# Softmax-window sums laid out as the image is, and the padding zeros of all images written early from another queue

## The chip, the cores and the metric

The kernel runs on one core of a Trainium2 chip. The metric is the device time of one execution in microseconds. The engines are called PE (matmul), DVE (vector), ACT (activations), POOL (GpSimd) and SP (which only issues DMAs here). Names such as L691 are lines of the kernel before.

## The reference

Two layers on x of shape (4, 16, 256, 256), each with a residual and a group norm in front of it (8 groups of two channels).

```python
# layer 0: x = x + L0(gn(x)); K = 5
out = conv3x3(h, conv_w) + conv_b                     # 16 -> 16*25 channels
weights = softmax(out.reshape(N, C, 25, H, W), axis=2)
y = einsum('ncuij,ncuij->ncij', unfold5x5(h), weights)
# layer 1: x = x + L1(gn(x)); a 3x3 KAN convolution
y = conv3x3(silu(h), base_weight.sum) + conv3x3(b_splines(h), (spline_weight * spline_scaler).sum) + bias_weight
```

In layer 0 each pixel and channel so needs a numerator (the sum over 25 taps of exp(logit) times the shifted h) and a denominator (the sum of the 25 exponentials). Both convolutions pad h with zeros.

## The kernel before

**Prologue.** The four images of x are read once for the group statistics (`bn_stats`, `group_stats`, whose L155 on POOL makes the reciprocal deviation), and bounds on the logits are taken. The weights are put in place by `prepare0` and `prepare1` (POOL: L471 and L472 copy the convolution's weights, L494 multiplies the spline's; ACT's `whi`, L474, and DVE's `wn`, L475, split one part in two). Image 0 is normalized here by the generator `normalize`, a step at a time between the statistics of the other images.

**What `normalize` writes.** It stores h three times into DRAM: `hs`, by strips with two rows and columns of padding, from which the shifted h is read; and `hst` and `hsl`, transposed by columns, from which the matmuls' operands are read. Its rows of zeros around h are DMAs of their own at the head of the generator: four into `hs` (L256), four into `hst` (L262) and four into `hsl` (L263), twelve for an image. Image 0's are issued from POOL's queue, in the prologue. Those of images 1, 2 and 3 are issued from SP's queue when layer 0 begins the image before, just ahead of the load of the first rows of x for the next image (`xp`, L276).

**Layer 0.** There are 64 strips: image, half of the rows (128 partitions), 32 columns. A strip has eight steps of four columns. In a step PE makes the logits of four columns (L791 with fp32 weights, L795 with the rest), ACT the exponentials into `e[:, 0]` (L814), POOL the products with h in `e[:, 1]` (L819), and DVE sums the 25 taps of both halves into `nd` (L691):

```python
nd = ndp.tile([P, 2, SW, C], F32, name=f"nd_{n}{arm}", tag="nd")
```

`nd` has three buffers and `e` four. After the last step of a strip, some steps later each, ACT computes a reciprocal of the denominators through Ln and Exp into the PSUM tile `r` (L704, L705), DVE corrects it by one Newton step (L709, L710) and multiplies the numerators by it (L713). This last multiply reads `nd` in its order, columns outside and channels inside, and writes the tile `o` in the order of x, channels outside:

```python
o = ndp.tile([P, C, SW], F32, name=f"o_{n}{arm}", tag="o", bufs=2)
nc.vector.tensor_mul(o.rearrange("p c j -> p j c"), nd[:, 1], r)
after(LAG + 3, apply, n, o, xc)
```

POOL subtracts `o` from x in `apply` (L719; the correction has the opposite sign), ACT takes statistics for layer 1 (L731), and every four strips ACT's queue stores the result (`x1s`). Between the steps of a strip run the steps of `normalize` for the next image: ACT normalizes, PE transposes, ACT copies, DVE subtracts (L366). Image 3 has no next image.

**Layer 1** follows; it computes splines on DVE and ACT and convolves on PE.

**What sets the order.** Within a layer the instructions of each engine are kept in the order of the program (`in_order`); in the prologue a scheduler orders them. SP's queue takes its DMAs in order, and so does POOL's, among POOL's arithmetic. A DMA waits for the one eight before it on the same kind of queue to land, as the two share a semaphore.

Of the kernel before, what the change touches and what calls it, by code (L numbers as in the profile page):

```python
# [11 lines left out]
F32 = mybir.dt.float32  # L12
# [21 lines left out]
def conv_preact_kernel(  # L34
# [12 lines left out]
    nc = tc.nc  # L47
    B, C, H, W = x.shape
    G = 8
    GC = C // G  # L50
    P = 128
    NH = H // P
# [3 lines left out]
    PAD = K // 2  # L56
    HP = H + 2 * PAD
    NS = 8
    EPS = 1e-5
    SW = 32  # L60
    NST = W // SW
    SP = SW + 2 * PAD
    CI = 8
    CX = 128
    JG = 4
    LAG = 1
    RP = P + 2
# [15 lines left out]
    hs = [dram.tile([NST, HP, C, SP], F32, name=f"hs{b}") for b in range(B)]  # L83
    hst = [[dram.tile([C, CT], F32, name=f"hst{b}_{h}") for h in range(NH)] for b in range(B)]

    hsl = [[dram.tile([C, 2, CT], F32, name=f"hsl{b}_{h}") for h in range(NH)] for b in range(B)]
# [38 lines left out]
    for r in range(RT):  # L125
        p = SROWS.index(r + 1) * C
# [115 lines left out]
    zero = const.tile([PAD * C, max(RP, NST * SP)], F32, name="zero")  # L242
# [2 lines left out]
    zpad = const.tile([P, QC, PAD], F32, name="zpad")  # L245
    nc.vector.memset(zpad, 0.0)

    def normalize(b, ptr, tiles, held=None, copier=None, queue=nc.sync):

        prep, xps, tts, his, los = tiles
        copier = copier or nc.scalar.copy
        for e in (0, HP - PAD):
            for r in range(PAD):
                queue.dma_start(  # L256
                    hs[b][:, e + r].rearrange("s c w -> c s w"),
                    zero[0:C, 0 : NST * SP].rearrange("c (s w) -> c s w", s=NST),
                )
        for h in range(NH):  # L260
            for w in (0, (W + 1) * RP):
                queue.dma_start(hst[b][h][:, w : w + RP], zero[0:C, 0:RP])  # L262
                queue.dma_start(  # L263
                    hsl[b][h][:, :, w : w + RP].rearrange("c t r -> (c t) r"), zero[:, 0:RP]
                )

        moves = []

        def move():
# [113 lines left out]
        for q in range(C // QC):  # L383
            ahead = rows(q + 1) if q + 1 < C // QC else iter(())
# [15 lines left out]
    with tc.tile_pool(name="prep0", bufs=2) as prep, tc.tile_pool(  # L400
        name="pre", bufs=1
    ) as pre, tc.tile_pool(
        name="xin", bufs=3
    ) as xin, tc.tile_pool(name="stat", bufs=2) as stat, tc.tile_pool(
        name="pstat", bufs=1, space=PSUM
    ) as pstat, tc.tile_pool(name="ptr0", bufs=3, space=PSUM) as ptr0:

        tiles = norm_tiles(prep)
        held = [pre.tile([P, C, W + 2 * PAD], F32, name=f"held{h}") for h in range(NH)]
# [15 lines left out]
        for dj in range(3):  # L425
            v = conv_wt[dj].rearrange("(d c) n -> c d n", d=3)
# [5 lines left out]
        v = conv_wt[2, 2 * C : 3 * C]  # L432
# [10 lines left out]
        for d in range(3):  # L443
# [3 lines left out]
            v = spl_s[dc]  # L447
# [73 lines left out]
        ahead = iter(())  # L521
        for b in range(B):
            st = stat.tile([P, G, NH * (GC if b == 0 else 1), 6], F32, name=f"st0_{b}", tag=f"st0{min(b, 1)}")
            for hf in range(NH):
                n = b * NH + hf
                t = loaded.pop(0)
                for g in range(G):
                    if b == 0:
                        for k in range(GC):
                            nc.vector.bn_stats(st[:, g, hf * GC + k, :], t[:, g * GC + k, :])  # L530
                    else:
                        nc.vector.bn_stats(
                            st[:, g, hf, :],
                            t[:, g * GC : (g + 1) * GC, :].rearrange("p c w -> p (c w)"),
                        )
                    next(ahead, None)
                    next(ahead, None)

                nc.scalar.activation(xq, t, AF.Square)
                sq = pstat.tile([P, W], F32, name=f"sq_{n}", tag="sq")  # L540
                for c in range(C):
                    nc.tensor.matmul(
                        sq, lhsT=idr, rhs=xq[:, c], start=c == 0, stop=c == C - 1
                    )
                nc.vector.tensor_reduce(hm[:, n : n + 1], sq, AX.X, ALU.max)
                next(ahead, None)
                if n >= NH and n + 3 < B * NH:
                    loaded.append(load_x(n + 3))
            mean, rstd = group_stats(stat, pstat, st, f"x{b}")
            nc.vector.tensor_copy(nrm[b][:, 0], rstd)  # L550
            nc.vector.scalar_tensor_tensor(nrm[b][:, 1], mean, -1.0, rstd, ALU.mult, ALU.mult)
            nc.gpsimd.tensor_mul(nrz[b][:, 0], rstd, gsel_sb)
            nc.vector.scalar_tensor_tensor(nrz[b][:, 1], rstd, EPS, rstd, ALU.mult, ALU.mult)
            ms = stat.tile([P, 2], F32, name=f"ms_{b}", tag="ms")
            nc.vector.tensor_mul(mean, mean, mean)
            nc.vector.tensor_reduce(ms[:, 0:1], mean, AX.X, ALU.add)
            nc.vector.tensor_scalar(ms[:, 0:1], ms[:, 0:1], 9.0 * GC, None, ALU.mult)
            nc.vector.tensor_reduce(ms[:, 1:2], rstd, AX.X, ALU.max)
            nc.vector.tensor_mul(ms[:, 1:2], ms[:, 1:2], ms[:, 1:2])
            v = hm[:, b * NH : (b + 1) * NH]  # L560
            nc.vector.tensor_scalar(v, v, 9.0 / 8.0, ms[:, 0:1], ALU.mult, ALU.add)
            nc.vector.tensor_scalar(v, v, ms[:, 1:2], None, ALU.mult)
            if b == 0:
                prepare0()
            if b == 1:
                prepare1()
            if b == 0:
                ahead = normalize(0, ptr0, tiles, held, nc.vector.tensor_copy, nc.gpsimd)
                next(ahead)
        for _ in ahead:  # L570
            pass
# [39 lines left out]
    def layer0(shift):  # L611

        arm = "g" if shift else ""
        marks = {}
        first = len(nc.cur_bb.bb.instructions)
        with tc.tile_pool(name=f"prep{arm}", bufs=2) as prep, tc.tile_pool(
            name=f"im{arm}", bufs=NIM
        ) as imp, tc.tile_pool(name=f"l0{arm}", bufs=2) as l0, tc.tile_pool(
            name=f"nd{arm}", bufs=3
        ) as ndp, tc.tile_pool(name=f"x1{arm}", bufs=3) as x1p, tc.tile_pool(name=f"ptr{arm}", bufs=1, space=PSUM) as ptr, tc.tile_pool(  # L620
            name=f"plog{arm}", bufs=3, space=PSUM
# [5 lines left out]
            tiles = norm_tiles(prep)  # L627
# [51 lines left out]
            def after(k, f, *args):  # L679

                later.append([k, partial(f, *args)])
# [7 lines left out]
            def sums():  # L689
                nd, j, e, done = waiting.pop(0)  # L690
                nc.vector.tensor_reduce(  # L691
                    nd[:, :, j : j + JG, :], e.rearrange("p t j m c d -> p t j c m d"),
                    AX.XY, ALU.add,
                )
                if done is not None:
                    done()

            def finish(n, nd, xc):
                after(LAG + 2, seed, n, nd, xc)


            def seed(n, nd, xc):
                r = prc.tile([P, SW, C], F32, name=f"r_{n}{arm}", tag="r")
                nc.scalar.activation(r, nd[:, 0], AF.Ln)  # L704
                nc.scalar.activation(r, r, AF.Exp, scale=-1.0)  # L705
                after(1, divide, n, nd, xc, r)

            def divide(n, nd, xc, r):
                nc.vector.tensor_mul(nd[:, 0], nd[:, 0], r)  # L709
                nc.vector.scalar_tensor_tensor(r, nd[:, 0], 2.0, r, ALU.subtract, ALU.mult)  # L710

                o = ndp.tile([P, C, SW], F32, name=f"o_{n}{arm}", tag="o", bufs=2)
                nc.vector.tensor_mul(o.rearrange("p c j -> p j c"), nd[:, 1], r)  # L713
                after(LAG + 3, apply, n, o, xc)

            def apply(n, o, xc):
                w0 = strips[n][2] * SW % CX
                v = xc[:, :, w0 : w0 + SW]
                nc.gpsimd.tensor_sub(v, v, o)  # L719
                if w0 + SW == CX:  # L720
                    for g in range(G):
                        after(1 + g, statistics, n, xc, g)
                    after(2, store, n, xc)
# [12 lines left out]
            def store(n, xc):  # L736
# [8 lines left out]
                    name=nc.get_next_instruction_name(), engine=mybir.EngineType.Activation,  # L745
# [8 lines left out]
            nxc, xc = load_xc(0), None  # L754
            ahead = iter(())
            for n, (b, hf, s) in enumerate(strips):
                if (hf, s) == (0, 0):
                    for _ in ahead:
                        pass
                    ahead = normalize(b + 1, ptr, tiles) if b + 1 < B else iter(())  # L760
# [8 lines left out]
                if s * SW % CX == 0:  # L769
                    xc = nxc  # L770

                nd = ndp.tile([P, 2, SW, C], F32, name=f"nd_{n}{arm}", tag="nd")
                for j in range(0, SW, JG):
                    if j % CI == 0:
                        k = n * nci + j // CI
# [10 lines left out]
                    e = l0.tile([P, 2, JG, K, C, K], F32, name=f"e_{n}_{j}{arm}", tag="e", bufs=LAG + 3)  # L786
                    for j1 in range(0, JG, 2):
                        lg = plog.tile([P, 2, 512], F32, name=f"lg_{n}_{j}_{j1}{arm}", tag="lg")
                        for i in range(2):
                            o = (j + j1 + i) % CI * RP  # L790
# [9 lines left out]
                        if shift:  # L800
                            mx = l0.tile([P, 2, C], F32, name=f"mx_{n}_{j}_{j1}{arm}", tag="mx")
                            for i in range(2):
                                v = lg[:, i, :NL].rearrange("p (m c d) -> p m c d", m=K, c=C)
# [3 lines left out]
                                w = bass.AP(  # L807
                                    tensor=mx.tensor, offset=mx.offset + i * C,
                                    ap=[mx.ap[0], [0, K], [1, C], [0, K]],
                                )  # L810
# [24 lines left out]
            while waiting:  # L835
                sums()
# [224 lines left out]
    with tc.If(fast > 0) as small_logits:  # L1061
        layer1("", *layer0(False))
    with small_logits.Else():
        layer1("g", *layer0(True))
# [42 lines left out]
```

## Time and profile before

| | us |
|---|---|
| median of 3 runs (lowest to highest) | 3093.68 (3092.81 to 3095.0) |
| the profiled execution | 3092.67 |
| its span | 3090.9 |
| of it: prologue, to the first reduce L691 | 135.8 |
| layer 0, first L691 to the last L713 | 135.8 to 2073 |
| layer 1 and the end | 2073 to 3091 |

The span is the time from the first to the last instruction of the profile. A group's row in the profile reads: line, engine, operation, tiles written and read, shapes and count; then busy time in us and mean ns of one; then the engine's idle time just before such instructions and what ended it. A timeline's row has start and duration in us, and in brackets the engine's idle time before it. SPq is SP issuing DMAs.

### The profile page before, as it was taken

How to read it: one execution, taken by the hardware profiler on the slowest of the kernel's cores; microseconds unless marked ns; L12 is line 12 of the kernel's file. 1: busy time of each engine (PE TensorE's matmuls, PEld its weight loads, DVE VectorE, ACT ScalarE, POOL GpSimd, SP SyncE). 2: the span in 40 equal slices, each digit the busy share in tenths (PEclk: the TensorE clock that was granted, in tenths of full speed). 3: DMA queues.
4: the chain of work that ended last, by engine and by line, in shares of the span. 5: the costliest groups of instructions: out<-in, count | busy, mean ns of one | idle time of the engine just before them, and what ended most of it. 6: DMA issues, size and time to landing. Idle time of an engine off the chain costs nothing.

```text
span 3090.9 us, 40797 instructions
## 1 busy us (share of the span) xinstructions
PE 2840.5 (92%) x14760; PEld 1484.6 (48%) x14760; DVE 2976.4 (96%) x1571; ACT 2240.5 (72%) x2619; POOL 1951.1 (63%) x734
## 2 busy tenths in 40 slices
PE   4499999989999999999999999957999999999998
PEld 3366656656556666666666566632222222222222
DVE  7499999999999999999999999988999999999997
ACT  6466665676766566756646546559999999999995
POOL 4199999999999999999999999970100100000000
PEclk7699999999999999999999999988999999999999
DMA  9988977879878778878867667649999988999994
GB/s 275 284 222 224 249 203 206 219 189 255 230 206 240 191 202 224 242 214 218 221 161 199 164 171 193 156 110 201 194 193 197 197 194 191 197 196 198 193 198 89
DMA packets 352725, 626.36 MB, mean 203 GB/s; under 512 B 41330, under 2 KB 218724, under 8 KB 336644
## 3 DMA queue, kind: packets, MB, share of 16 engines
q1 hardware_dynamic: 318020, 605.29, 79.0%
q10 hardware_dynamic: 33024, 16.78, 1.9%
q8 instruction: 121, 1.98, 0.3%
q0 software_dynamic: 1472, 1.59, 0.2%
q14 instruction: 88, 0.72, 0.1%
HBM read 513.95 MB, written 104.24 MB: 200 GB/s over the span
## 4 chain that ended last, share of the span: by engine, by line
DVE 65%; PE 9%; ACT 9%; issue 8%; DMA 6%; SPq 2%; POOL 1%; DVEq 0%; ACTq 0%; POOLq 0%
DVE nd L691 45%; PE yp L988 3%; PE lg L791 3%; DVE ta L169 3%; DVE ta L168 3%; DVE tb L169 3%; DVE tb L168 3%; DMA sx<-x1s 2%; DVE ring L170 2%; DVE o L713 1%; DVE tb L159 1%; DVE r L710 1%; DMA an<-hsl 1%; ACT sl L924 1%; ACT ta L167 1%
## 5 line engine op out<-in xcount | busy, mean ns | idle before, releaser
L791 PE MATMUL lg<-wm,am 128*128 128x400 f32 x4096 | 1741.2, 506 | 102.9 <-ACT e L814 64.2
L819 POOL TENSOR_TENSOR e<-e,u 128x1600 f32<-128x1600 f32 x512 | 1789.9, 3547 | 67.7 <-ACT e L814 48.6
L691 DVE TENSOR_REDUCE nd<-e 128x128 f32<-128x3200 f32 x512 | 1746.9, 3476 | 31.6 <-POOL e L819 31.5
L795 PE MATMUL lg<-wn,an 97*128 97x400 f32 x2048 | 1349.7, 659 | 12.1 <-DMA an<-hsl 11.9
L814 ACT ACTIVATE e<-lg 128x800 f32<-128x800 f32 x1024 | 817.8, 837 | 726.4 <-DVE nd L691 522.3
L791 PEld LDWEIGHTS lg<-wm,am 128*128 128x128 f32 x4096 | 764.3, 193 | 424.1 <-ACT e L814 113.3
L988 PE MATMUL yp<-ring,wt 128*32 128x512 f32 x6144 | 739.7, 595 | 66.8 <-POOL ring L959 46.5
L795 PEld LDWEIGHTS lg<-wn,an 97*128 97x128 f32 x2048 | 389.3, 190 | 330.3 <-issue 21.1
L988 PEld LDWEIGHTS yp<-ring,wt 128*32 128x32 f32 x6144 | 206.9, 109 | 591.5 <-issue 470.0
L905 POOL MEMSET sx<- 16x256 f32 x8 | 2.4, 302 | 667.2 <-PE yp L996 232.5
L1004 PE MATMUL yp<-sl,ws 64*32 64x512 f32 x1536 | 176.5, 588 | 0.0
L731 ACT ACTIVATE z<-xc,nrm 128x256 f32<-128x256 f32 x256 | 153.6, 600 | 10.5 <-POOL xc L719 6.2
L170 DVE SCALAR_TENSOR_TENSOR ring<-ta,ta 128x2048 f32<-128x2048 f32 (+1 forms) x64 | 147.8, 2309 | 10.8 <-ACT z L731 8.3
L169 DVE TENSOR_TENSOR ta<-ta,ta 128x2048 f32<-128x2048 f32 (+1 forms) x64 | 148.4, 2318 | 2.9 <-ACT ta L167 2.9
L170 DVE SCALAR_TENSOR_TENSOR ring<-tb,tb 128x2048 f32<-128x2048 f32 x64 | 145.6, 2276 | 2.6
L169 DVE TENSOR_TENSOR tb<-tb,tb 128x2048 f32<-128x2048 f32 x64 | 145.2, 2268 | 0.7 <-ACT tb L167 0.7
L924 ACT ACTIVATE sl<-sx,q 64x2048 f32<-64x2048 f32 x64 | 133.4, 2085 | 1.5 <-DMA sx<-x1s 1.4
L194 POOL TENSOR_TENSOR d<-d,nrz 128x8 f32<-128x8 f32 x4 | 2.7, 663 | 200.1 <-DVE d L192 200.1
L167 ACT ACTIVATE ta<-ta 128x2048 f32<-128x2048 f32 (+1 forms) x64 | 123.2, 1925 | 2.0
L167 ACT ACTIVATE tb<-tb 128x2048 f32<-128x2048 f32 x64 | 120.5, 1883 | 0.0
L1004 PEld LDWEIGHTS yp<-sl,ws 64*32 64x32 f32 x1536 | 48.8, 106 | 116.2 <-issue 115.9
L719 POOL TENSOR_TENSOR xc<-xc,o 128x512 f32<-128x512 f32 x64 | 85.0, 1328 | 13.4 <-DVE o L713 13.4
(181 smaller groups left out, 2054.3 us busy)
## 6 DMA issues: line engine op xcount, KB each, us to landing
am<-hst SPq DMA_DIRECT2D x512, 194.6 KB
u<-hs SPq DMA_DIRECT2D x320, 288.0 KB
an<-hsl SPq DMA_DIRECT2D x512, 129.8 KB
xta<-x1s SPq DMA_DIRECT2D x40, 1024.0 KB
xtb<-x1s SPq DMA_DIRECT2D x40, 1024.0 KB
xtc<-x1s SPq DMA_DIRECT2D x40, 1024.0 KB
am<-hst SPq DMA_DIRECT2D x256, 129.8 KB
sx<-x1s SPq DMA_DIRECT2D x248, 128.0 KB
```

The source lines that it names most:

```text
L167: nc.scalar.activation(s1, r1, AF.Square, scale=2.0)
L168: nc.vector.scalar_tensor_tensor(s2, t, 2.0, s2, ALU.subtract, ALU.mult)
L169: nc.vector.tensor_mul(s1, s1, r1)
L170: nc.vector.scalar_tensor_tensor(f, s2, 0.0, s1, ALU.min, ALU.subtract if given else ALU.add)
L691: nc.vector.tensor_reduce(nd[:, :, j : j + JG, :], e.rearrange("p t j m c d -> p t j c m d"), AX.XY, ALU.add,)
L791: nc.tensor.matmul(lg[:, i, :NL], lhsT=am[:, o : o + P], rhs=wm.rearrange("p m c d -> p (m c d)"), start=True, stop=False,)
L795: nc.tensor.matmul(lg[:, i, :NL], lhsT=an[:, o : o + P], rhs=wn.rearrange("p m c d -> p (m c d)"), start=False, stop=True,)
L814: nc.scalar.activation(ev, lg[:, :, :NL], AF.Exp)
L819: nc.gpsimd.tensor_tensor(e[:, 1].rearrange("p j m c d -> p j (m c) d"), e[:, 0].rearrange("p j m c d -> p j (m c) d"), uv, ALU.mult,)
L924: nc.scalar.activation(sl[n % 2][:, :, 1 : W + 1], t, AF.Silu, scale=sc[b][0][0 : RD * C], bias=sc[b][1][0 : RD * C],)
L988: nc.tensor.matmul(yp[t * M : (t + 1) * M], lhsT=wt[:, d, e].rearrange("p r o -> p (r o)"), rhs=ring[:, r0 + t * RT + d : r0 + t * RT + d ...
L1004: nc.tensor.matmul(yp[t * M : (t + 1) * M], lhsT=ws[:, e].rearrange("p r o -> p (r o)"), rhs=sl[n % 2][:, t : t + NT + 1 : NT, e : e + W], ...
```

## The change

`nd` is laid out as channels by columns, as x is, and so is `r`. L691 then writes its sums, which it still makes column by column, 32 elements apart. The last multiply runs in place in `nd`, `o` is gone, and `apply` reads `nd[:, 1]`. Apart from this, the zeros become a function of their own, `zeros(b)`, called in the prologue for each of the four images after its statistics and ahead of `prepare0` and `prepare1`, and all issued from POOL's queue.

```diff
+    def zeros(b):
+
         for e in (0, HP - PAD):
             for r in range(PAD):
-                queue.dma_start(
+                nc.gpsimd.dma_start(
                     hs[b][:, e + r].rearrange("s c w -> c s w"),
                     zero[0:C, 0 : NST * SP].rearrange("c (s w) -> c s w", s=NST),
                 )
         for h in range(NH):
             for w in (0, (W + 1) * RP):
-                queue.dma_start(hst[b][h][:, w : w + RP], zero[0:C, 0:RP])
-                queue.dma_start(
+                nc.gpsimd.dma_start(hst[b][h][:, w : w + RP], zero[0:C, 0:RP])
+                nc.gpsimd.dma_start(
                     hsl[b][h][:, :, w : w + RP].rearrange("c t r -> (c t) r"), zero[:, 0:RP]
                 )
 
+    def normalize(b, ptr, tiles, held=None, copier=None):
...
+            zeros(b)
             if b == 0:
                 prepare0()
             if b == 1:
                 prepare1()
             if b == 0:
-                ahead = normalize(0, ptr0, tiles, held, nc.vector.tensor_copy, nc.gpsimd)
+                ahead = normalize(0, ptr0, tiles, held, nc.vector.tensor_copy)
...
                 nc.vector.tensor_reduce(
-                    nd[:, :, j : j + JG, :], e.rearrange("p t j m c d -> p t j c m d"),
+                    nd[:, :, :, j : j + JG].rearrange("p t c j -> p t j c"),
+                    e.rearrange("p t j m c d -> p t j c m d"),
                     AX.XY, ALU.add,
                 )
...
-                r = prc.tile([P, SW, C], F32, name=f"r_{n}{arm}", tag="r")
+                r = prc.tile([P, C, SW], F32, name=f"r_{n}{arm}", tag="r")
...
-                o = ndp.tile([P, C, SW], F32, name=f"o_{n}{arm}", tag="o", bufs=2)
-                nc.vector.tensor_mul(o.rearrange("p c j -> p j c"), nd[:, 1], r)
-                after(LAG + 3, apply, n, o, xc)
-
-            def apply(n, o, xc):
+                nc.vector.tensor_mul(nd[:, 1], nd[:, 1], r)
+                after(LAG + 3, apply, n, nd, xc)
+
+            def apply(n, nd, xc):
                 w0 = strips[n][2] * SW % CX
                 v = xc[:, :, w0 : w0 + SW]
-                nc.gpsimd.tensor_sub(v, v, o)
+                nc.gpsimd.tensor_sub(v, v, nd[:, 1])
...
-                nd = ndp.tile([P, 2, SW, C], F32, name=f"nd_{n}{arm}", tag="nd")
+                nd = ndp.tile([P, 2, C, SW], F32, name=f"nd_{n}{arm}", tag="nd")
```

More of the change, by code (lines that the diff above doesn't have):

```diff
@@ L246, in conv_preact_kernel @@
     nc.vector.memset(zpad, 0.0)
-    def normalize(b, ptr, tiles, held=None, copier=None, queue=nc.sync):
-        prep, xps, tts, his, los = tiles
-        copier = copier or nc.scalar.copy
+    def zeros(b):
         for e in (0, HP - PAD):
             for r in range(PAD):
-                queue.dma_start(
+                nc.gpsimd.dma_start(
                     hs[b][:, e + r].rearrange("s c w -> c s w"),
@@ L261, in normalize @@
             for w in (0, (W + 1) * RP):
-                queue.dma_start(hst[b][h][:, w : w + RP], zero[0:C, 0:RP])
-                queue.dma_start(
+                nc.gpsimd.dma_start(hst[b][h][:, w : w + RP], zero[0:C, 0:RP])
+                nc.gpsimd.dma_start(
                     hsl[b][h][:, :, w : w + RP].rearrange("c t r -> (c t) r"), zero[:, 0:RP]
                 )
+    def normalize(b, ptr, tiles, held=None, copier=None):
+        prep, xps, tts, his, los = tiles
+        copier = copier or nc.scalar.copy
         moves = []
```

## The prediction

> **What bounds the kernel now.** I read the page first (busy times, then the slices), then the windows view by stage, then the groups with their shapes apart, and last the timelines of single engines where a stage begins.
>
> ```profile
> PE 2840.5 (92%) x14760; PEld 1484.6 (48%) x14760; DVE 2976.4 (96%) x1571; ACT 2240.5 (72%) x2619; POOL 1951.1 (63%) x734
> DVE  7499999999999999999999999988999999999997
> ...
> 200.00:600.00 400.00, 381.31 (x1346) 247.21 (x1345) 399.11 (x161) 254.63 (x447) 388.95 (x121) 0.99 0.82 219
> 1660.00:2060.00 400.00, 373.82 (x1275) 238.79 (x1273) 398.57 (x168) 221.74 (x342) 397.84 (x132) 0.98 0.66 170
> ```
>
> The third column of busy times in a window is DVE, the fifth POOL. Layer 0 runs from about 136 to 2074 us, 64 strips. In images 0 to 2 (first window) DVE is busy 399.11 of 400 us and POOL 388.95: DVE is the bound, POOL 2.5% behind it. In image 3 (second window) both are full. So DVE time in layer 0 is worth its face value only as far as POOL lets it; layer 1 (2120 us to the end) is not touched.
>
> The groups with their shapes show what DVE does in a strip:
>
> ```profile
> L819 POOL TENSOR_TENSOR e<-e,u 128x1600 f32<-128x1600 f32 x512 | 1789.9, 3547 | 67.7 <-ACT e L814 48.6 <-DMA an<-hsl 9.2 <-DMA u<-hs 3.8
> L691 DVE TENSOR_REDUCE nd<-e 128x128 f32<-128x3200 f32 x512 | 1746.9, 3476 | 31.6 <-POOL e L819 31.5
> L713 DVE TENSOR_TENSOR o<-nd,r 128x512 f32<-128x512 f32 x64 | 69.3, 1083 | 2.2
> L709 DVE TENSOR_TENSOR nd<-nd,r 128x512 f32<-128x512 f32 x64 | 43.6, 681 | 3.2 <-ACT r L705 3.2
> ```
>
> L713 and L709 multiply the same two kinds of operand (nd from SBUF, r from PSUM) over 512 elements. L713 alone writes across its order, and takes 1083 ns for 681.
>
> [...] The DVE timeline gives L713 to the next instruction as 0.91 us, and L366, a like multiply whose follower doesn't need its result, as 0.59:
>
> ```profile
> 2026.97 1.07 DVE L713 TENSOR_TENSOR o<-nd,r 128x512 f32<-128x512 f32 x1
> 2027.88 3.46 DVE L691 TENSOR_REDUCE nd<-e 128x128 f32<-128x3200 f32 x1
> ...
> 898.13 0.69 DVE L366 TENSOR_TENSOR lo<-tp,hi 128x512 fp32r<-128x512 f32 x1
> 898.72 3.48 DVE L691 TENSOR_REDUCE nd<-e 128x128 f32<-128x3200 f32 x1
> ```
>
> Over layer 0 the median spacings are L713 0.922, L366 0.598, L691 3.393, POOL's L819 3.482 and L719 1.234 us.
>
> The stage's start has a stall of its own, seen in three engines' timelines:
>
> ```profile
> 135.87 3.18 SPq L256 DMA_DIRECT2D hs<-zero  x4
> 143.62 0.98 SPq L276 DMA_DIRECT2D xp<-in_x_dram  x2
> ...
> 147.91 0.87 ACT L323 ACTIVATE hsp<-xp,nrm 128x576 f32<-128x576 f32 x1 [12.32 <-DMA xp<-in_x_dram]
> ...
> 150.30 3.51 POOL L819 TENSOR_TENSOR e<-e,u 128x1600 f32<-128x1600 f32 x1 [11.07 <-ACT e L814]
> ```
>
> SP spends 135.87 to 143.6 on image 1's twelve zero writes; only then does it issue the xp load. ACT, in order, waits 12.32 us for xp and holds the exponentials (L814) behind it; POOL then idles 11.07, DVE 11.10, PE 9.70 us. This is on the path.
>
> [...] (922 - 598) / 512 = 0.63 ns[...]. [...] 3393 ns for 3200 inputs, 1.06 ns each. So L691 is paced by inputs, and emits one output in 25. [...] POOL's L819 stays within 3503 to 3637 ns beside it. [...] the trace has 5.0 to 6.4 us to landing for the zeros that POOL issues today, and I use that.
>
> **The change part by part.**
>
> (a) *L713 in order.* It becomes L709's form without a dependent follower: 0.922 to 0.598, 0.324 us, 64 times: -20.7 us of DVE in layer 0. L709, L710, L704 and L705 stay contiguous on both sides. L719 reads nd[:, 1] instead of o, with the same steps: nothing.
>
> How much of this arrives? A strip costs DVE 8 x 3.393 + 0.71 + 0.73 + 0.922 = 29.51, plus 0.60 for each L366 (none to two per strip, 48 in layer 0); POOL 8 x 3.482 + 1.234 = 29.09. So POOL gains 0.42 us a strip on DVE, and 0.6 more with an L366. After: 29.18 against 29.09, a gain of 0.09. Setting the two timelines side by side, POOL's product lies at least 3.3 to 3.9 us ahead of its reduce at best; stops of the matmuls for their loads (strips 10, 18, 26, 34, 42, 53) eat that lead, down to 0.1, 0.0, 1.7, 0.0, 0.0 and 0.0, and DVE idles only 1.75 (strip 18) and 0.4 us (strip 54). With the slower refill: strips 11 to 18 have 5 L366, 5 x 0.6 + 8 x 0.09 = 3.7; 34 and 42 are refilled by 5 and 11 L366; 43 to 53 by 4, 3.4. The lead's ceiling (four e buffers) falls by the same 0.3. So each of five stops costs some 0.4 more: 2.2 us given back. Net **-18.5**; unknown between -20.7 (stops absorbed) and -8 (stops half as large again drain the lead each time).
>
> (b) *L691 writes 128 bytes apart instead of side by side.* Not in the trace. Bounds: nothing, if one output in 25 inputs leaves the write time; or the hop's 0.63 ns for each of 128 outputs, 81 ns, x 512 = +41 us. A gain is excluded: the inputs set the pace. I take **0**: with 26 ns between outputs there is room for one 0.63 ns hop.
>
> (c) *Zeros leave SP.* 36 issues leave SP's queue, 5.6 us at 614.7 and 1098.3 and 7.7 at 135.9. The later two stall nobody (PE waits only for e there): 0. At 135.9 xp can be issued 7.7 us earlier, but the DMA engines are full until about 139.5 (shares 1.10 and 0.87 in 136 to 140, then 0.15), and xp took 4.3 us from issue to landing, much of it transfer. From 139.5 it lands near 142.7 instead of 147.9: **-5.2**, between -3 and -7.7. Late next is then the PE, which already runs without gap from 150 to 182. Freed semaphores shift the DMAs' slots, but the wait behind the x1s stores falls to the same loads (u or an), so the stops stay.
>
> (d) *Zeros on POOL in the prologue.* 36 more issues at 0.50 to 0.54 us, 19 us of POOL, but each waits for the one eight back to land: 8 per 5.7 us, 0.71 each, 26 us. POOL was idle 45.5 to 57.1, 59 to 74 and 76 to 105 us, so there is room. In the order of the built program, image 1's twelve follow 37.85, to 46.4, with the wm copies (43.44 today) at 45 among them; then L494 (37.87 today) 47.4 to 50.4, then the wp copies (44.42) to 51.4; ACT's whi moves behind the square of the fourth input (54.8 us) and DVE's wn to just before L153, so 51.4 is in time. Seven of image 2's precede the second L155: 51.4 + 5 = 56.4 for 57.12. The remaining 17 precede the third: 59 + 12 = 71 for 74.17. Margins of 0.7 and 3 us are thin while landings take 5 to 7 us; behind L155 wait DVE's nrm and the statistics queued after it. I take **+1.5**, between 0 and +5. The traffic, 36 x 8 to 18 KB, is half a MB of small packets where the DMA share is 0.65: nothing.
>
> (e) *nd is held until L719 instead of L713; o goes.* nd lives some 17 of 24 steps that its three buffers allow: no wait.
>
> **Sum.** -18.5 + 0 - 5.2 + 1.5 = -22.2. The profiled execution took 3092.67 us (span 3090.9); the median of the runs is 3093.68, 1.0 more. 3093.7 - 22.2 = **3071.5**.
>
> **The rivals.** *The reduce pays for its hops*: [...] For it: nothing in the trace writes a reduce so. Against it: the 26 ns between outputs. +41.5 - 18.5 - 5.2 + 1.5 = +19, 3113. It decides from (18.5 + 5.2 - 1.5) / 512 = 43 ns per reduce; it ends slower. *POOL and the loads become the bound*: the second window has POOL at 397.84 of 400, and the loads' stops grow in step. Then (a) brings 8, (c) 5.2, and (d) costs 3: 3083.5. *The prologue gives back the start*: landings of 8 us make the second and third L155 late and (d) costs 5 instead of 1.5: 3075. *The change doesn't shorten L713* (the hop was not the reason): speaks against it that L709 has the same operands; 3090, no change.
>
> **How the numbers follow.** A measurement of this kernel tells 0.2% (6.2 us) from no change. Forecast with its bounds, the late prologue included (3063 to 3079): 0.62. POOL and the loads (3078 to 3087): 0.22. Near no change (L713 or mixed small losses): 0.06. Reduce slower: 0.10. Range 3063 to 3087, chances 0.84, 0.06, 0.10.
>
> **What would show it.** L713's successor at about 681 ns (1083 before); L691 still 3476 and 3393 apart; SP's xp load near 136 us, ACT's wait there near 7 us; L155 at 57, 74 and 105 us or later; DVE idle in layer 0 under 5 us after the first strip. A reduce above 3520 ns, or DVE idling 10 us before L691 behind POOL, would make the prediction wrong.

## The result, and the profile after

The changed kernel takes 3072.44 us (median of 4 runs, 3070.19 to 3072.6) against 3093.24 for the kernel before beside it, a ratio of 0.993 (95% interval 0.9913 to 0.9948). In a second set of runs it was 3075.74 against 3093.05 (5 and 9 runs), 0.9945 (0.9931 to 0.9958). So it is faster by 17 to 21 us; 22.2 had been forecast. The profiled executions compared below took 3092.67 us before and 3072.59 after.

First the groups with their shapes apart, of the changed kernel (count, then busy us and mean ns of one, then the idle time ahead and what ended it). L691 has become L694, L709 L713, L713 L715, L819 L821, L719 L721:

```profile
L821 POOL TENSOR_TENSOR e<-e,u 128x1600 f32<-128x1600 f32 x512 | 1788.7, 3539 | 46.3 <-ACT e L816 30.9 <-DMA an<-hsl 11.8 <-DVE nd L694 3.1
L694 DVE TENSOR_REDUCE nd<-e 128x128 f32<-128x3200 f32 x512 | 1748.0, 3478 | 26.7 <-POOL e L821 26.5
L715 DVE TENSOR_TENSOR nd<-nd,r 128x512 f32<-128x512 f32 x64 | 43.9, 686 | 2.2
L713 DVE TENSOR_TENSOR nd<-nd,r 128x512 f32<-128x512 f32 x64 | 43.3, 677 | 3.2 <-ACT r L709 3.2
```

The multiply fell from 1083 to 686 ns, level with its twin L713. The reduce, whose writes now lie 128 bytes apart, went from 3476 to 3478. The DVE timeline gives L715 to the next start as 0.61 us, for 0.91. Costs are counted from start to start, as durations reach past the next start: this multiply's is 0.69 us, and was 1.07.

```profile
2008.88 0.69 DVE L715 TENSOR_TENSOR nd<-nd,r 128x512 f32<-128x512 f32 x1
2009.49 23.84 DVE L694 TENSOR_REDUCE nd<-e 128x128 f32<-128x3200 f32 x7
```

Where layer 0 starts, the timelines of three engines answer to the three shown before:

```profile
140.93 0.97 SPq L278 DMA_DIRECT2D xp<-in_x_dram  x2
...
147.84 0.87 ACT L325 ACTIVATE hsp<-xp,nrm 128x576 f32<-128x576 f32 x1 [7.52 <-DMA xp<-in_x_dram]
...
150.24 3.52 POOL L821 TENSOR_TENSOR e<-e,u 128x1600 f32<-128x1600 f32 x1 [6.27 <-ACT e L816]
```

ACT's wait shrank from 12.32 to 7.52 us, POOL's from 11.07 to 6.27. Yet ACT starts at 147.84 where it started at 147.91: the wait is shorter because everything ahead of it is later. POOL's timeline shows that in the prologue's last L155 (104.85 before):

```profile
110.11 1.64 POOL L155 TENSOR_TENSOR rstd_x<-var_x,mhalf 128x8 f32<-128x8 f32 x1 [33.33 <-DVE var_x L153]
```

So three marks divide the difference of the two profiled executions. The first reduce of strip 1 starts at 176.0 us (175.8 before): +0.2. From there to the first reduce of strip 63 pass 1843.7 us (1862.3): -18.6. From there to the end, 1051.1 (1052.8): -1.8. So in these two executions layer 0 gives the gain, and the zeros gained at the start of layer 0 what they had lost in the prologue.

### The profile page after: what moved, and what is told of

It is laid out like the page before. It is cut to its first block, busy times and chain, and to the rows that moved or that the text cites. A ratio compares the mean times of both kernels' runs of the same rounds, so it can differ in the third digit from the quotient of the medians.

```text
span 3070.7 us, 40813 instructions
## 1 busy us (share of the span) xinstructions
PE 2830.4 (92%) x14760; PEld 1479.7 (48%) x14760; DVE 2953.9 (96%) x1571; ACT 2239.5 (73%) x2619; POOL 1970.2 (64%) x770
## 4 chain that ended last, share of the span: by engine, by line
DVE 63%; PE 12%; issue 8%; ACT 8%; DMA 6%; SPq 1%; POOL 1%; DVEq 0%; ACTq 0%; POOLq 0%
DVE nd L694 43%; PE lg L793 6%; PE yp L990 3%; DVE ta L169 3%; DVE tb L169 3%; DVE tb L168 3%; DVE ta L168 3%; PE lg L797 2%; DVE ring L170 2%; DVE tb L159 1%; DVE r L714 1%; DMA xin<-in_x_dram 1%; DVE yo L973 1%; DMA an<-hsl 1%; DVE nd L713 1%
## 5 line engine op out<-in xcount | busy, mean ns | idle before, releaser
L821 POOL TENSOR_TENSOR e<-e,u 128x1600 f32<-128x1600 f32 x512 | 1788.7, 3539 | 46.3 <-ACT e L816 30.9
L694 DVE TENSOR_REDUCE nd<-e 128x128 f32<-128x3200 f32 x512 | 1748.0, 3478 | 26.7 <-POOL e L821 26.5
L721 POOL TENSOR_TENSOR xc<-xc,nd 128x512 f32<-128x512 f32 x64 | 84.7, 1323 | 11.0 <-DVE nd L715 11.0
```

Source lines behind the costliest of these rows:

```text
L694: nc.vector.tensor_reduce(nd[:, :, :, j : j + JG].rearrange("p t c j -> p t j c"), e.rearrange("p t j m c d -> p t j c m d"), AX.XY, ALU.add,)
L821: nc.gpsimd.tensor_tensor(e[:, 1].rearrange("p j m c d -> p j (m c) d"), e[:, 0].rearrange("p j m c d -> p j (m c) d"), uv, ALU.mult,)
```

## The experiments

Two questions were open: what each half of the change does alone, and why the prologue is 5 us later. For the second there were two theories. **Q**: POOL's queue makes the copies of wp late, ACT then waits for DVE's wn (2.20 us at 56.91), SP's stores and, behind them, the input loads slip. **P**: the zeros' small writes take DMA time from the input loads, wherever they stand.

The table gathers what all runs showed. "Prologue" is the start of the last L155; "start" is from POOL's first product (L821) to the first reduce of strip 1; "strips" from there to the first reduce of strip 63; all from the profiled execution, in us. That one need not be the median: in e4, e6, e9 and e10 it was the slowest of its kernel's runs. The last column is the median against that of the kernel before beside it.

| kernel | sums | zeros of images 1 to 3 | prologue | start | strips | median, against before |
|---|---|---|---|---|---|---|
| before | old | SP, ahead of xp | 104.9 | 43.5 | 1862.3 | |
| after | new | POOL, in the prologue | 110.1 | 39.0 | 1843.7 | 3072.44, -20.8 |
| after_again | new | the same | 108.8 | 41.7 | 1844.3 | 3075.74, -17.3 |
| e1_layout | new | SP, ahead of xp | 105.9 | 45.3 | 1843.7 | 3076.18, -16.7 |
| e2_zeros | old | POOL, in the prologue | 109.9 | 39.2 | 1863.1 | 3090.78, -2.1 |
| e3_zeros_sp_late | new | SP, spread behind xp | 105.4 | 41.8 | 1843.7 | 3069.96, -22.9 |
| e3_again | new | the same | 106.2 | 39.3 | 1848.7 | 3072.54, -21.3 |
| e4_zeros_behind_wp | new | POOL, behind the wp copies | 110.0 | 41.8 | 1846.7 | 3075.10, -17.7 |
| e5_zeros_pool_end | new | POOL, behind the last L155 | 105.2 | 38.4 | 1844.7 | 3073.24, -19.8 |
| e8_wp_late | new | as e3; wp copied late | 105.1 | 39.1 | 1846.8 | 3070.78, -22.3 |
| e9_zeros_between | new | POOL, where they hold up nothing | 111.1 | 41.5 | 1848.6 | 3075.57, -17.5 |
| e10_xp_first | new | as e3; xp issued early | 105.6 | 37.1 | 1847.6 | 3067.51, -26.2 |

**One half at a time.** e1 is the kernel before with only the order of `nd`, `r` and the sums changed, e2 the kernel before with only the zeros moved:

```diff
 e1:  -nd = ndp.tile([P, 2, SW, C], F32, ...)   +nd = ndp.tile([P, 2, C, SW], F32, ...)
      (with L691, r and the last multiply as in the change)
 e2:  +zeros(b)   in the prologue's loop, on nc.gpsimd
```

> The order of the sums alone; the zeros stay on SP, image by image. My theory: the multiply's shorter spacing carries the whole gain, and the zeros' move nets to nothing, because what SP saves at the start of layer 0 (4.8 us) is lost in the prologue (4.7 us). Then this kernel takes 3072 to 3075 us, the last L155 is at about 105 us, ACT waits about 12 us for xp again, and the first full strips run at the same absolute time as in both kernels. Rival, that the zeros carry a part of the gain as the prediction's sum has it (3.7 us net): 3076 to 3078 us.

> The zeros' move alone; sums in the old order. My theory: the prologue ends about 4.7 us later (last L155 at about 110 us) and layer 0's start gains about 4.8 us (ACT waits 7 to 8 us for xp), so 3092 to 3094 us, no change. The prediction's sum, gain 5.2 and loss 1.5: 3089 to 3090 us. A third way, that the prologue's delay has nothing to do with the zeros: last L155 at about 105 us and 3088 us.

e1 took 3076.18 us (5 runs; 0.9945, 0.9931 to 0.9958), e2 3090.78 (13 runs; 0.9994, 0.9986 to 1.0002). e1's strips take what the changed kernel's take, to 0.1 us, and e2's what those of before take, to 0.8: the order of the sums alone makes the difference in layer 0. The zeros alone are worth -2 us with an interval from -4.3 to +0.6, which leaves both no change and the forecast's -3.7 standing. e2's time lies between its first two expectations; e1's lies in the range of the rival, that the zeros carry a part of the gain, but its interval covers both. In e1's profile ACT waited 15.13 us for xp, not 12, and strip 1 came 2.3 us later than in the changed kernel. What e2's profile does show is both halves of the exchange: prologue 5.1 us later, start 4.4 us shorter.

**Queue or packets.** e4 holds the 36 writes on POOL behind the wp copies. e9 goes further: image 1's behind those copies, the others' behind the third L155. e8 is the converse, with no zeros of images 1 to 3 in the prologue, but with POOL kept busy so that wp is late. The edits, shortened:

```diff
 e4:  +behind(i, copied)          # i: each zero DMA; copied: the last wp copy on POOL
 e9:  +zeros(1, copied)           # and images 2 and 3 behind the third L155's product:
      +zeros(2, newest(POOL)); zeros(3, newest(POOL))
 e8:  +7 x nc.gpsimd.memset(idle, 0.0)    # between the copies of wm and of wp, in e3
```

> The changed kernel, with the 36 zero writes of images 1 to 3 held on GpSimd behind the copies of the normalised weights (wp), which then start near 45 us as before the change. Theory Q (the queue): the prologue is late because those copies wait in GpSimd's queue and ACT waits 2.2 us for what DVE makes of them, so SP's stores and input loads slip; then ACT's wait is gone, the last L155 comes back to about 105 us, and the time is 3067 to 3069 us. Theory P (the packets): the zeros' small writes take DMA time from the input loads wherever they stand; then the last L155 stays near 110 us and the time near 3072 us. Between: the zeros now reach past 70 us on GpSimd, and the third L155 (74 us) may start late by up to 4 us.

> The changed kernel with the zeros where GpSimd's queue holds nothing up: those of image 1 behind the wp copies, those of images 2 and 3 behind the third L155 (74 us). wp is then copied near 45 us and the third L155 starts at 74 to 75 us, but all 36 writes still fall among the input loads. Q: last L155 at 105 to 106 us, and 3067 to 3069 us. P: the packets still cost DMA time; last L155 at 108 to 110 us and 3071 to 3073 us.

> The kernel e3 (zeros of images 1 to 3 on SP behind the xp load, so none in the prologue) with GpSimd kept busy for some 6 us between the copies of wm and of wp, so that wp is copied near 50 us as in the changed kernel, without any zero packet. Q: ACT waits about 2 us for wn, the stores and the input loads slip, and the last L155 comes at 108 to 110 us and the time 2 to 4 us above e3. P: the last L155 stays at 105 to 106 us and the time at e3's.

e4 came out at 3075.10 us with the last L155 at 110.0, against Q; but in it the zeros also held up the third L155 (77.6 us for 74.2), so alone it settles nothing. e9 has neither delay, though its time, 3075.57, is above what P expected. ACT's wait for wn in e9 is gone, the third L155 stands where it should, and still the last one is late. The lines are of ACT's and POOL's timelines:

```profile
54.99 0.50 ACT L495 CAST wn<-wp 32x400 fp32r<-32x400 f32 x1
...
74.58 1.66 POOL L155 TENSOR_TENSOR rstd_x<-var_x,mhalf 128x8 f32<-128x8 f32 x1 [12.78 <-DVE var_x L153]
...
111.07 1.66 POOL L155 TENSOR_TENSOR rstd_x<-var_x,mhalf 128x8 f32<-128x8 f32 x1 [20.18 <-DVE var_x L153]
```

e8 has the late wp without the packets. It is late enough for ACT to wait (1.24 us rather than the 2 intended), and the last L155 is on time:

```profile
56.33 0.53 ACT L503 CAST wn<-wp 32x400 fp32r<-32x400 f32 x1 [1.24 <-DVE wn L502]
...
105.14 1.64 POOL L155 TENSOR_TENSOR rstd_x<-var_x,mhalf 128x8 f32<-128x8 f32 x1 [29.48 <-DVE var_x L153]
```

Over all kernels the two groups don't touch: the last L155 stands at 104.9 to 106.2 us where no zeros of images 1 to 3 are written among the input loads (7 profiles), and at 108.8 to 111.1 where they are (6, e6 below among them). So the zeros' writes are enough to bring the delay (e9), and P holds as far as that. The late wp of Q is not needed for it, and in e8 a wait of 1.24 us brought no delay of the last L155. That the wait of 2.20 us in the changed kernel adds a part is not excluded: SP's first store behind it is issued 1.4 us later than before (59.82 us for 58.43), 0.8 in e8.

What the packets take is in the DMA view of 40 to 110 us (packets, MB, share of the time of 16 engines; POOL's writes are q0, SP's q1). First the changed kernel, then e3, then e9:

```profile
DMA packets 19873, 19.42 MB, mean 277 GB/s; under 512 B 1758, under 2 KB 16053, under 8 KB 19869
...
q1 hardware_dynamic: 18584, 18.81, 83.3%
q0 software_dynamic: 1285, 0.57, 5.1%
```

```profile
q1 hardware_dynamic: 20253, 20.61, 91.8%
q0 software_dynamic: 144, 0.06, 0.4%
```

```profile
q1 hardware_dynamic: 18495, 18.69, 83.0%
q0 software_dynamic: 1285, 0.57, 6.1%
```

The zeros are half a MB, but 4.7% of 70 us, 3.3 us of all 16 engines; in e9 5.7%, 4.0 us. That is 130 to 160 GB/s, where q1 has 323. The trace's record of each packet tells more. Half of POOL's 1285 packets are of 4 bytes and take some 10 ns each. The others are of 520 and 1040 bytes, which take 36 and 66 ns (SP's of 576 and 1024 bytes take 33 and 49), and of 1152 bytes, the rows of `hs`. These last, 192 packets, take 146 ns each, and 199 in e9: alone they are 1.75 us of the 16 engines, and 2.4. SP's packets of 2080 bytes take 94 ns in the changed kernel's window, so size alone does not explain the slow ones. (In `hs` the strips lie apart, so a packet of 1152 bytes goes to eight places of 144 bytes; whether that makes it slow, no run here shows.) In what order the engines serve the two queues isn't shown either.

The DMA engines' time is not the whole of it. SP issues the loads of the inputs in one queue with the stores of image 0's h. Its last load of an input, before, in the changed kernel and in e9:

```profile
83.84 0.63 SPq L419 DMA_DIRECT2D xin<-in_x_dram  x1
...
88.73 0.64 SPq L421 DMA_DIRECT2D xin<-in_x_dram  x1
...
89.00 0.60 SPq L438 DMA_DIRECT2D xin<-in_x_dram  x1
```

The same two groups of profiles part here: this issue ends at 84.5 to 85.1 us in the seven and at 88.7 to 89.6 in the six. Where ACT waits for this load, it gets it 8.9 and 9.1 us later in e10 and e5, and 9.1 to 9.2 later in after, after_again and e2. So in these three the whole delay is there when the load is issued, and the load itself hardly takes longer; in e4, e6 and e9 it also takes longer, 9.8 to 10.5 us. In e9 SP needs 16.0 us from the store at 73.03 to that load, in e3 11.4 for the same stores. The windows view shows the DMA engines less full for it, not fuller (before, then the changed kernel; the last two columns are their share and GB/s):

```profile
60.00:70.00 10.00, 4.14 (x19) 3.64 (x17) 10.00 (x23) 8.49 (x9) 0.00 (x0) 0.50 1.02 328
80.00:90.00 10.00, 6.07 (x31) 5.51 (x30) 5.37 (x13) 8.42 (x13) 0.00 (x0) 0.70 1.05 341
...
60.00:70.00 10.00, 2.32 (x11) 2.32 (x12) 10.00 (x28) 9.55 (x13) 7.52 (x15) 0.64 0.89 259
80.00:90.00 10.00, 6.25 (x28) 5.76 (x28) 8.54 (x18) 8.81 (x12) 0.00 (x0) 0.67 0.92 324
```

From 40 to 110 us q1 moved 1.8 MB less in the changed kernel than in e3. So the zeros delay SP's stores, and the load behind these comes late. A store waits for the DMA eight before it to land: the one at 79.88 us in the changed kernel waits 3.1 us for the input load issued at 68.05 (2.3 us before, at 74.97 for 64.13). Slower landings would so delay the stores; that it is this wait, and not SP's issuing itself, was not measured.

**Other places for the zeros.** e3 leaves them on SP, one every second step, behind the xp load. e5 leaves them on POOL, behind the prologue's end.

```diff
 e3:  +moves.extend((4 + 2 * i, partial(nc.sync.dma_start, *z)) for i, z in enumerate(zero_dmas()))
 e5:  +zeros(b, done)        # after the prologue's loop; done: POOL's last instruction there
```

> Sums in the new order; the zeros of images 1 to 3 stay on SP's queue, but one at a time, each two steps after another, behind the xp load of their image instead of ahead of it. The prologue is then that of the kernel before and the xp load comes as early as in the changed kernel. If gain and loss are what I think, last L155 at about 105 us, xp issued near 136 us, ACT's wait about 7 us, and 3067 to 3069 us. Rival: the start of layer 0 is bound by something else (the full DMA engines until 139.5 us), the xp load lands no earlier, and the time is 3072 us as with the change. It would be above 3074 us if the spread issues delay SP's later loads.

> The changed kernel with the zeros of images 1 to 3 on GpSimd's queue behind the prologue's last GpSimd instruction (the last L155 and its product), so that none is written while the inputs load. Both theories of the late prologue, the queue (Q) and the packets (P), expect last L155 back at 105 us. From there 36 issues of 0.52 us take GpSimd to about 126 to 131 us, ahead of its first product near 132 us. If the start of layer 0 is bound by DMA throughput, the zeros' packets (some 3.5 us of all 16 engines by the changed kernel's trace) delay the first loads, and the time is 3071 to 3073 us, nothing gained on the changed kernel; if they find room, 3067 to 3069 us.

e3 took 3069.96 us (0.9925, 0.9912 to 0.9939), near the first expectation; but its ACT waited 12.51 us for xp, not the 7 expected, and started the normalization only at 147.25 us, 9.5 us after xp's issue at 137.73. e5 has the prologue back (105.2), but POOL's issues run into the start: its first product comes at 137.2 us instead of 132 to 133, and 3073.24 us lies just above what was expected for a start bound by DMA.

> The changed kernel once more, on the same chip as the runs beside it: 20 to 21 us below the kernel before, last L155 at about 110 us, first full strips at about 176 us.

> The kernel e3 once more (sums in the new order, zeros of images 1 to 3 spread on SP behind the xp load): 22 to 24 us below the kernel before, as in its first five runs, and so 2 to 5 us below the changed kernel. If its first runs were a lucky start of layer 0: 18 to 20 us below.

after_again came in at -17.3 us, a smaller gain than expected, and its strip 1 at 178.5 us. e3_again took 3072.54 (0.993, 0.9916 to 0.9943), between its two expectations, and in it DVE waited longer for POOL in strips 34 and 42 (strips 1848.7 us, 5 more than the first time). So the gain of one kernel differs by up to 3.5 us from one set of runs to another, and the start by 3 us between profiles; what is concluded above rests on the timelines, not on such differences.

**The xp load.** With no zeros ahead of it, xp took 6.9 us from SP's issue to ACT's start in the changed kernel, 9.1 in after_again, 9.5 in e3 and 7.1 in e3_again, against 4.3 before and 4.5 in e1. The windows view of the kernel before, then of the changed one, says why (the last two columns are the share of the DMA engines and GB/s):

```profile
140.00:145.00 5.00, 0.00 (x0) 0.00 (x0) 2.75 (x1) 0.00 (x0) 0.00 (x0) 0.91 0.17 29
```

```profile
140.00:145.00 5.00, 4.59 (x17) 2.77 (x15) 4.48 (x2) 0.33 (x1) 3.97 (x2) 1.00 1.11 254
145.00:150.00 5.00, 0.51 (x1) 0.50 (x2) 2.49 (x1) 2.15 (x3) 0.00 (x0) 0.81 1.10 289
```

While SP issued zeros, the engines ran nearly dry, and xp was then issued into them. Without the zeros xp is issued into full engines, behind xc (1 MB) and the third am and an. e10 puts xp ahead of those in e3:

```diff
+ahead = normalize(1, ptr, tiles)
+next(ahead)                    # issues image 1's first xp loads
 nxc, xc = load_xc(0), None     # then xc, then am and an in the first strip
```

> The kernel e3 with image 1's first xp load issued ahead of the xc load and of the third am and an load, instead of behind them (some 8 us earlier on SP); the normalisation of image 1 runs one step earlier. My theory of what was mis-sized in the prediction: without the zeros in front, xp is issued while the DMA engines are full of xc, am and an, and takes 7 to 9.5 us to land instead of 4.3. Then xp lands before about 141 us here, ACT's wait falls from 7.7 to 12.5 us to under 3 us, strip 1 starts at 168 to 171 us instead of 172 to 174.5, and the time is 3066 to 3069 us. Rival, that the loads now behind xp end last in its place (the third am and an, or xc): ACT or PE waits as long for those, and the time is e3's, 3070 to 3073 us.

It took 3067.51 us (3066.91 to 3071.31, 5 runs; 0.9919, 0.9906 to 0.9933), the lowest median of all: 26 us below the kernel before. Its interval overlaps those of e3 and of the changed kernel, though, so that the time alone does not set it apart. ACT's wait:

```profile
137.94 0.87 ACT L328 ACTIVATE hsp<-xp,nrm 128x576 f32<-128x576 f32 x1 [5.58 <-DMA xp<-in_x_dram]
```

ACT starts 7 to 9 us earlier than in e3 (144.71 and 147.25 us), but its wait was meant to fall below 3 us and is 5.58. Strip 1 starts at 170.7 us, as expected; yet it starts at 172.1 and 174.5 in the two profiles of e3 and at 171.1 in e8, which differs from e3 by the late wp alone. So a gain from the earlier xp is not clear of the differences between profiles. In e10 PE now waits 1.96 us for an am that went behind (the rival's way). That xp meets full engines is seen in the windows; that its place in the queue is worth some us is not shown.

**The reduce's hops, and the next bound.** e7 puts reduces on scratch tiles ahead of everything; e6 leaves out L715.

```diff
 e7:  +for d in (25, 8, 4, 2):        # v: d inputs for each of 128 outputs
      +    for _ in range(6):
      +        nc.vector.tensor_reduce(near, v, AX.X, ALU.add)
      +    for k in range(6):
      +        nc.vector.tensor_reduce(
      +            to[:, :, :, 4 * k : 4 * k + 4].rearrange("p t c j -> p t j c"), v, AX.X, ALU.add
      +        )
 e6:  -nc.vector.tensor_mul(nd[:, 1], nd[:, 1], r)
```

> The changed kernel with reduces ahead of everything else, on scratch tiles that nothing later reads: 128 outputs from 25, 8, 4 and 2 inputs each, six times with the outputs side by side and six times with them 128 bytes apart, as L694 has them after the change. My theory (the inputs set the pace, a hop hides behind them): equal starts for both at 25 and 8 inputs, about 3390 and 1090 ns apart; a difference, if at all, only at 2 inputs, where an output falls due every 2.1 ns, and then at most 81 ns. Rival (each hop adds its 0.63 ns whatever the inputs): 81 ns more for the spread form at every size. The whole kernel takes some 80 us longer than the changed one; that time says nothing else.

> The changed kernel without L715: the sum itself instead of its product with r is subtracted from xc, so DVE has 64 x 0.605 = 38.7 us less to do in layer 0 and the result is another one. If GpSimd has become as good as co-bound (29.10 us a strip against 29.19 on DVE, plus 0.60 for each L368), most strips are then GpSimd's, no lead is rebuilt after a stop, and the time is 3042 to 3055 us, a half to four fifths of the saving. Rival, that DVE is still the only bound: all of it, 3033 to 3036 us.

e7's groups (near side by side, to 128 bytes apart):

```profile
L91 DVE TENSOR_REDUCE to<-ti 128x128 f32<-128x3200 f32 x6 | 20.9, 3476 | 0.0
L89 DVE TENSOR_REDUCE near<-ti 128x128 f32<-128x3200 f32 x6 | 20.8, 3468 | 0.0
...
L91 DVE TENSOR_REDUCE to<-ti 128x128 f32<-128x256 f32 x6 | 2.5, 410 | 0.0
L89 DVE TENSOR_REDUCE near<-ti 128x128 f32<-128x256 f32 x6 | 2.4, 408 | 0.0
```

(The 3468 holds one of 3428, the very first; the others are 3474 to 3477.) From start to start both forms take 3392 to 3394 ns at 25 inputs, the first two apart, and 326 to 327 at 2; with 1127 and 593 at 8 and 4 that is 1.04 ns for each further one of the 256 to 3200 inputs, so the inputs set the pace. Even at 2 inputs an output, the hop costs no more than about 1 ns in 128 outputs, so the rival's 81 ns falls at every size.

e6 took 3052.2 us (4 runs; 0.9858, 0.9843 to 0.9873), within the expected 3042 to 3055. Its strips take 1830.9 us: 12.7 us less, though L715 had cost 62 x 0.605 = 37.5 there. DVE's idle time ahead of the reduces shows the rest:

```profile
L694 DVE TENSOR_REDUCE nd<-e 128x128 f32<-128x3200 f32 x512 | 1754.2, 3480 | 53.0 <-POOL e L820 52.7
```

53.0 us of idling for 26.7, behind POOL. So this further cut of DVE in layer 0 brought about a third of its face value there. Some 5 us of e6's gain lie behind strip 63; they were not traced.

## Why the prediction was right, and where it was not

The time was forecast as 3071.5 us, 22.2 below the profiled execution, and came 20.1 below it. The total fits better than its parts: (c) and (d) were to bring -3.7 together and brought +0.2 in these two profiles, and the -1.8 behind strip 63, which was not forecast, makes good about half of that. So much of the closeness is luck; the gain in (a) is not.

- **(a) Right, and its exactness chance.** Adding up the time from each DVE start to the next over strips 1 to 62, idle time apart: the two multiplies by r together fell from 99.5 to 79.6 us, -19.9, or 0.32 for each strip as worked out (the last one takes 0.606 for the 0.598 forecast). DVE's idle time ahead of the reduces stayed, 2.2 and 2.3 us: the 2.2 us that longer stops were to give back were not given back in this pair. Over the eleven profiles of the complete new order (e7 among them) it is 2.0 to 6.8 us, 4.0 on average, against 2.2 and 2.8 in the two of the old. Nearly all of it falls in strips 18, 26, 34, 42 and 54, at stops that the prediction names. So the term was of the right kind, and 1.5 us on average for 2.2, and with it the strips' gain varies from 13.6 to 18.6 us in the table.
- **(b) Nearly right.** In the same sum the reduces went from 3392.3 to 3394.8 ns on average, 2.5 ns each, 1.3 us in 496. All eleven profiles of the complete new order have 3394.5 to 3396.3, the two of the old one 3392.3 and 3392.7. In e7's test, with PE idle and ACT and POOL little used (4.2 and 12.9 of 60 us), the difference is at most about 1 ns. So the writes' order costs 2 to 4 ns in layer 0; why only there stays open, as the test also reads its inputs in another pattern. -19.9 + 1.3 is the -18.6 found, where the forecast had -18.5. The price for a hop, in the prediction 0.63 ns an element from the spacings of 922 and 598 ns, held for the multiply, 0.62 here. That each output of a reduce would pay it, as the rival has it, was an estimate, and it did not carry over.
- **(c) A gain of the right kind, on average a little too large.** With the zeros ahead of xp the start takes 43.5 and 45.3 us (before, e1), with them gone 38.4 to 41.8 (eleven profiles, e7 and e6 among them; e10 apart): some 4 us for 5.2. In the changed kernel's own profile xp took 6.9 us from issue to ACT's start, close to the 6.8 that the forecast implies, and ACT's wait of 7.52 is close to the 7 named. What is too good is "from 139.5 it lands near 142.7": the prediction took full engines into account, but only until 139.5, where the profile before has them run dry since SP issued nothing but zeros. With these gone the share is still 1.1 up to 150 us in the changed kernel, and in other kernels xp took up to 9.5.
- **(d) Mis-sized: +4.7 for +1.5** (by POOL's first product, 136.97 us for 132.23). The margin at the second L155 held and that at the third nearly (57.04 and 74.83 for 57.12 and 74.17). What failed is the sentence "half a MB of small packets where the DMA share is 0.65: nothing". The 0.65 is the mean of 40 to 60 us in the kernel before; some 44% of these packets go out after 60 us, where its share is 1.02, and where SP's loads wait behind its stores. In the changed kernel SP issues the last load 4.9 us later. The delay shows where that input is squared, on ACT's timeline (93.46 before, without a wait):

```profile
98.59 3.62 ACT L541 ACTIVATE xq<-xin 128x4096 fp32r<-128x4096 f32 x1 [4.29 <-DMA xin<-in_x_dram]
```

- **(e)** `nd` held longer made no wait: the idle time stayed. The rival "the prologue gives back the start" names what happened in size, but by a late second and third L155, which isn't how it came: only the last one was late.
- The rest, -1.8 us behind strip 63, was not forecast. The last strip's multiplies and those still due account for under 1 us of it; the profiles of the new order differ there by 1.2 us.

## What to carry to other kernels

Before moving "free" DMAs into another stage, look at the DMA engines' share in that very stretch and not in a mean over two stretches, and ask what waits there for loads: small writes from one engine's queue can make another's loads late, as SP's last input load was here, by 4 to 5 us. Reckon with the time that such packets take in the trace, not with their bytes. A shorter wait in the profile is no gain until its end is compared in absolute time. And when a wait behind SP's issues is removed, the engines may have been idle only because of that wait; the load's time must then be taken from full ones (here 6.9 to 9.5 us from issue to ACT's start, for 4.3 and 4.5 in the nearly idle ones).

## What was not expected of the hardware

- A reduce with single outputs 128 bytes apart starts its follower as soon as one with outputs side by side, at 25, 8, 4 and 2 inputs an output (3393, 1127, 593 and 327 ns for 128 outputs), while a multiply with one output for each input paid 0.62 ns each.
- 36 DMAs of 8 to 18 KB, 0.51 MB in all, held the 16 DMA engines for 3.3 to 4.0 us, two to two and a half times as long as SP's packets need for the same bytes. More than half of that time went to 192 packets of 1152 bytes, at 146 to 199 ns each, where SP's packets of 1024 bytes took 49.
- These writes, issued by POOL, made SP issue its last input load 4 to 5 us later, while the DMA engines' share fell (0.89 for 1.02 from 60 to 70 us, 0.92 for 1.05 from 80 to 90).
